# Attention probabilities transposed by VectorE blocks and small transfers instead of TensorE

## The chip, the cores and the metric

The kernel runs on one core of one Trainium2 chip (trn2). The core has five engines with their own instruction streams: TensorE (PE; its weight loads are listed apart as PEld), VectorE (DVE), ScalarE (ACT), GpSimd (POOL) and SyncE (SP), which here only issues transfers. TensorE reads SBUF and writes PSUM. The metric is the device time of one execution in microseconds (us), lower is better; a change counts as faster or slower when it moves that time by over 2%.

## The reference, cut to what matters

There are 64 graphs of 256 nodes with 512 features, all float32, and two layers. Layer 0 is gated attention with 8 heads of 64 channels; layer 1 is a graph attention with one head. The change concerns layer 0.

```python
x:   (64, 256, 512) float32      adj: (64, 256, 256) int32

h = relu(layernorm(x))
q, k, v = (h @ Wq.T), (h @ Wk.T), (h @ Wv.T)          # split into 8 heads of 64
scores = einsum('bqhd,bkhd->bhqk', q, k) / sqrt(64)
scores = where(adj != 0, scores, -inf)
attn = softmax(scores, axis=-1)                       # 256 x 256 per head and graph
c = einsum('bhqk,bkhd->bqhd', attn, v)                # <- needs attn with k on the partitions
gate = sigmoid(concat([c, h]) @ Wg.T + bg)
x = x + gate * h + (1 - gate) * c
# layer 1
h = relu(layernorm(x)); Wh = h @ W
e = leaky_relu(Wh @ a1 + (Wh @ a2).T);  e = where(adj == 0, -1e9, e)
x = x + elu(softmax(e) @ Wh)
```

The softmax runs along a row, so a query lies on a partition and the keys along it. The product with v sums over the keys, so TensorE wants the keys on the partitions: each 256 x 256 matrix of probabilities has to be transposed between the two.

## The kernel before

Projections are done by a seven-product Strassen scheme (products into three PSUM banks `ma`, `mb`, `mc`, added up by VectorE with the help of `u` tiles). The work is pipelined over graphs: round `i` works on the attention of graph `i`, on the projections of graph `p = i+1`, on the gate of graph `q = i-1` and on layer 1 of graphs `q` and `r = i-2`. The order of TensorE and SyncE is the program order; that of the other engines is chosen by a scheduler when the program is built, and is fixed then too. The heads are handled in two halves of four.

```python
sb pools (buffers): ... "e": 4 [128 x 2 x 256], "eT": 4 [128 x 2 x 256], "adj": 1, "h": 1 ...
ps pools (PSUM banks): "ma": 1, "mb": 1, "mc": 1, "w": 5

def to_channels(h, name, pool):                # h of layer 0: VectorE blocks, 16 transfers per graph
    for t in range(NT):
        nc.vector.transpose(h[:, t, :], h[:, t, :])
    ...
    for i in range(0, P, 32):
        for j in range(0, P, 32):
            nc.sync.dma_start(placed[j:j + 32, :, i:i + 32], blocks[i:i + 32, :, j:j + 32])

def a_scores(g, half):                         # 16 TensorE instructions "ps" into 4 banks
    ...
def a_softmax(g, half, jj):                    # two heads; VectorE: scale, mask, row minimum;
    for i in range(2):                         # ScalarE: exp and row sum
        for t in range(NT):
            nc.vector.tensor_tensor_reduce(e[:, t, :], psc[jj, i][:, t, :], mask[:, t, :], ...)
            nc.scalar.activation(e[:, t, :], e[:, t, :], AF.Exp, ...)
    nc.vector.reciprocal(rec, sums)
    for i in range(2):                         # GpSimd: divide by the sum
        for t in range(NT):
            nc.gpsimd.tensor_scalar(es[jj, i][:, t, :], es[jj, i][:, t, :], rec[:, i, t:t + 1], ...)

def transpose_probs(e, pool, name, on_act):    # one head: 4 TensorE transposes, one copy
    pt = ps["w"].tile([P, NT, N], F32, ...)
    for kc in range(NT):
        for t in range(NT):
            nc.tensor.transpose(pt[:, kc, t * P:(t + 1) * P], e[:, t, kc * P:(kc + 1) * P], ident)
    eT = pool.tile([P, NT, N], F32, ...)
    evac(eT, pt, on_act)                       # ScalarE for layer 0

def a_weigh(g, half):                          # "pc": probabilities times v
    for jj in range(2):
        for kc in range(NT):
            for i in range(2):
                nc.tensor.matmul(pc[i * DK:(i + 1) * DK, jj, :], v[...], eT[jj, i][:, kc, :], ...)

def emit_round(i):                             # order of one round, cut
    load_graph(p+1); gate(q) part 0; softmax(i, 0, 1); edges(r); gate(q) part 1; sums(p)
    gate(q) part 2; mix(q); transpose(r); a_transpose(i, 0)
    qk(p) part 0; residual(q); out(r, 0); norm(q); qk(p) part 1
    a_scores(i, 1); softmax(i, 1, 0); out(r, 1); softmax(i, 1, 1); qk(p) part 2
    transpose_h(q); v(p) part 0; a_weigh(i, 0); v(p) part 1; stats(p+1)
    a_transpose(i, 1); v(p) part 2; wh(q) part 0; norm(p+1); p_transpose(p+1)
    a_weigh(i, 1); wh(q) part 1; a_scores(p, 0); softmax(p, 0, 0); wh(q) part 2
```

Tiles and their names in the profile: `ps` scores, `e` probabilities, `ptr` their transposes in PSUM, `eT` the same in SBUF, `pc` the product with v, `hT_l<-h_l` the 16 transfers of `to_channels`, `pma_/pmb_/pmc_` the Strassen banks, `py` and `pt_l` other transposes, `po` the product of layer 1, `S_l`, `S_g`, `S_c` sums of inputs for the Strassen scheme (GpSimd).

Of the kernel before, what the change touches and what calls it, by code (L numbers as in the profile page):

```python
# [8 lines left out]
F32 = mybir.dt.float32  # L9
I32 = mybir.dt.int32  # L10
BF16 = mybir.dt.bfloat16
AF = mybir.ActivationFunctionType
ALU = mybir.AluOpType
# [5 lines left out]
HUGE = 3e38  # L19
# [3 lines left out]
def kernel(  # L23
# [27 lines left out]

    nc = tc.nc
    B, N, H = x.shape
    NH = 8
    DK = H // NH
    P = 128
    HC = H // P
    NT = N // P  # L60
    HH = H // 2
    SCALE = 1.0 / DK ** 0.5
    assert N == 256 and H == 512 and SCALE == 0.125

    def pool(name, bufs, **kw):
        return ctx.enter_context(tc.tile_pool(name=name, bufs=bufs, **kw))
# [1 line left out]
    const = pool("const", 1)  # L68
    st = pool("st", 4)
    sb = {tag: pool(tag, bufs) for tag, bufs in {  # L70
        "x": 5, "adj": 1, "mask": 4, "hT": 3, "S": 3, "qk": 3, "v": 2, "wh": 1, "e": 4, "eT": 4,
        "cT": 1, "z": 1, "h": 1, "tmp": 6, "U": 3,
    }.items()}
    ps = {tag: pool(f"ps_{tag}", bufs, space=bass.MemoryType.PSUM) for tag, bufs in {
        "ma": 1, "mb": 1, "mc": 1, "w": 5,
    }.items()}

    ident = const.tile([P, P], F32, name="ident")
# [21 lines left out]
    def weight_sums(key):  # L100

        w = weight[key]
        t = const.tile([P, 3, 2, w.shape[3]], F32, name=f"w{key}_t")
        b11, b12, b21, b22 = (w[:, r:r + 2, n, :] for r in (0, 2) for n in range(2))
        nc.vector.tensor_tensor(t[:, 1], b22, b12, ALU.subtract)
        nc.vector.tensor_tensor(t[:, 0], t[:, 1], b11, ALU.add)
        nc.vector.tensor_tensor(b12, b12, b11, ALU.subtract)
        nc.vector.tensor_tensor(t[:, 2], b21, t[:, 0], ALU.subtract)
        weight[key] = {1: b11, 2: b21, 3: b22, 4: t[:, 2], 5: b12, 6: t[:, 0], 7: t[:, 1]}
# [21 lines left out]
    def evac(dst, src, on_act):  # L131
        if on_act:
            nc.scalar.copy(dst, src)  # L133
        else:
            nc.vector.tensor_copy(dst, src)  # L135
# [80 lines left out]
    def to_channels(h, name, pool):  # L216


        for t in range(NT):
            nc.vector.transpose(h[:, t, :], h[:, t, :])  # L220
        hT = pool.tile([P, NT, HC, P], F32, tag="t", name=f"hT_{name}")
        blocks = h.rearrange("p t (c q) -> p (t c) q", q=P)
        placed = hT.rearrange("p t c q -> p (t c) q")
# [3 lines that stand above are left out]
        return hT  # L227
# [23 lines left out]

    def p_transpose(g):
        s = graphs[g]
        s["hT"] = to_channels(s.pop("h"), f"l0_{g}", sb["hT"])

    def p_sums(g):
        s = graphs[g]
# [36 lines left out]
    def a_scores(g, half):  # L294
        s = graphs[g]
        qk = s["qk"][half]
        psc = {}
        for jj in range(2):
            for i in range(2):
                psc[jj, i] = ps["w"].tile([P, NT, N], F32, tag="t", name=f"ps_{g}_{half}_{jj}_{i}")  # L300
            for t in range(NT):
                for i in range(2):
                    r = i * DK
                    nc.tensor.matmul(  # L304
                        psc[jj, i][:, t, :], qk[r:r + DK, 0, jj, t * P:(t + 1) * P], qk[r:r + DK, 1, jj, :],
                        start=True, stop=True,
                    )
        s["ps"] = psc

        s["e", half] = {}  # L310

    def a_softmax(g, half, jj):
        s = graphs[g]
        psc, mask, es = s["ps"], s["mask"], s["e", half]
        low, sums, rec = (
            st.tile([P, 2, NT], F32, tag=tag, name=f"{tag}_{g}_{half}_{jj}") for tag in ("low", "sums", "rec")
        )
        for i in range(2):
            e = es[jj, i] = sb["e"].tile([P, NT, N], F32, tag="t", name=f"e_{g}_{half}_{jj}_{i}")
            for t in range(NT):  # L320
                nc.vector.tensor_tensor_reduce(  # L321
                    e[:, t, :], psc[jj, i][:, t, :], mask[:, t, :], -SCALE, HUGE, ALU.add, ALU.min,
                    accum_out=low[:, i, t:t + 1],
                )
                nc.scalar.activation(  # L325
                    e[:, t, :], e[:, t, :], AF.Exp, bias=low[:, i, t:t + 1], scale=-1.0,
                    accum_out=sums[:, i, t:t + 1],
                )
        nc.vector.reciprocal(rec, sums)  # L329
        for i in range(2):  # L330
            for t in range(NT):
                nc.gpsimd.tensor_scalar(  # L332
                    es[jj, i][:, t, :], es[jj, i][:, t, :], rec[:, i, t:t + 1], 1.0, ALU.mult, ALU.mult
                )

    def transpose_probs(e, pool, name, on_act):

        pt = ps["w"].tile([P, NT, N], F32, tag="t", name=f"ptr_{name}")
        for kc in range(NT):
            for t in range(NT):  # L340
                nc.tensor.transpose(pt[:, kc, t * P:(t + 1) * P], e[:, t, kc * P:(kc + 1) * P], ident)  # L341
        eT = pool.tile([P, NT, N], F32, tag="t", name=f"eT_{name}")
        evac(eT, pt, on_act)
        return eT

    def a_transpose(g, half):
        s = graphs[g]
        s["eT", half] = {
            (jj, i): transpose_probs(e, sb["eT"], f"{g}_{half}_{jj}_{i}", 1) for (jj, i), e in s.pop(("e", half)).items()
        }  # L350

    def a_weigh(g, half):
        s = graphs[g]
        eT = s.pop(("eT", half))
        if half == 0:
            s["cT"] = sb["cT"].tile([P, NT, HC, P], F32, tag="t", name=f"cT_{g}")
        pc = ps["w"].tile([P, 2, N], F32, tag="t", name=f"pc_{g}_{half}")
        for jj in range(2):
            for kc in range(NT):
                for i in range(2):  # L360
                    hd = 4 * half + 2 * jj + i
                    nc.tensor.matmul(  # L362
                        pc[i * DK:(i + 1) * DK, jj, :], s["v"][:, kc, hd * DK:(hd + 1) * DK], eT[jj, i][:, kc, :],
                        start=(kc == 0), stop=(kc == NT - 1),
                    )
        evac(
            s["cT"][:, :, 2 * half:2 * half + 2, :].rearrange("p t j q -> p j t q"),
            pc.rearrange("p j (t q) -> p j t q", q=P), 1,
        )
        if half:  # L370
            s["cS"] = token_sums(s["cT"], f"c_{g}")
# [77 lines left out]

    def g_transpose(g):  # L450
        s = graphs[g]
        s["egT"] = transpose_probs(s["eg"], sb["tmp"], f"l1_{g}", 0)

    def g_out(g, t):
        s = graphs[g]
# [17 lines left out]
    def emit_round(i):  # L473


        parts = {}

        def step(fn, g, *args):
            if 0 <= g < B:
                fn(g, *args)  # L480

        def part(fn, g, n):
            if 0 <= g < B:
                if n == 0:
                    parts[fn] = fn(g)
                parts[fn][n]()

        p, q, r = i + 1, i - 1, i - 2
        step(load_graph, p + 1)
        part(g_gate, q, 0)  # L490
        step(a_softmax, i, 0, 1)
        step(g_diff, q)
        step(g_edges, r)
        part(g_gate, q, 1)
        step(p_sums, p)
        part(g_gate, q, 2)
        step(g_mix, q)
        step(g_transpose, r)
        step(a_transpose, i, 0)
        if i == -1:  # L500
            weight_sums("q")
            weight_sums("k")
        part(p_qk, p, 0)
        step(g_residual, q)
        step(g_out, r, 0)
        step(g_norm, q)
        part(p_qk, p, 1)
        step(a_scores, i, 1)
        step(a_softmax, i, 1, 0)
        step(g_out, r, 1)  # L510
        step(a_softmax, i, 1, 1)
        part(p_qk, p, 2)
        step(g_transpose_h, q)
        if i == -1:
            weight_sums("v")
        part(p_v, p, 0)
        step(a_weigh, i, 0)
        if i == 0:
            weight_sums("gh")
            weight_sums("gc")  # L520
            nc.vector.tensor_scalar_mul(hbg, hbg, 0.5)
        part(p_v, p, 1)
        step(p_stats, p + 1)
        step(a_transpose, i, 1)
        part(p_v, p, 2)
        if i == 0:
            edge_columns()
            weight_sums("1")
        part(g_wh, q, 0)
        step(p_norm, p + 1)  # L530
        step(p_transpose, p + 1)
        step(g_sums, i)
        step(a_weigh, i, 1)
        part(g_wh, q, 1)
        step(a_scores, p, 0)
        step(a_softmax, p, 0, 0)
        part(g_wh, q, 2)
# [49 lines left out]
```

## Time and profile before

The time is 3592.71 us, the median of three runs (3591.24 to 3593.61). The profiled execution has a span of 3590.0 us.

| engine | busy, us | share of the span | instructions |
|---|---|---|---|
| PE | 3529.6 | 98% | 25984 |
| PEld | 3072.2 | 86% | 25984 |
| DVE | 1960.6 | 55% | 5673 |
| ACT | 1607.4 | 45% | 4289 |
| POOL | 1626.9 | 45% | 2439 |

The clock granted to TensorE is 0.995 of full speed in the mean, and below nine tenths in the last of 40 slices alone. The 16 DMA engines are busy some 10 to 20% of the time and move 128.74 MB. A page of the profile gives such sums; which engine sets the end is read from the chain of waits, and where the time of one stage goes is read from the timeline of one round. A round is the same sequence 64 times over, with a start and an end in which parts of it are missing.

### The profile page before, as it was taken

The numbers are of one execution on the slowest core, as the hardware profiler recorded it, in microseconds if no ns is written. First come the engines' busy times: TensorE is split into PE (matmuls) and PEld (weight loads), VectorE is DVE, ScalarE is ACT, GpSimd is POOL, SyncE is SP. The second block draws the span as 40 slices with busy tenths as digits, with TensorE's granted clock in tenths as the row PEclk, the third lists the DMA queues.
The fourth block names the chain that finished last, engine by engine and source line by source line (L and its number), as shares of the span: only waits on it lengthen the run. The fifth ranks groups of instructions, "written<-read, shape, count | busy, mean of one in ns | idle before, by whom it ended". The sixth has DMA issues, their size and how long they took to land.

```text
span 3590.0 us, 68740 instructions
## 1 busy us (share of the span) xinstructions
PE 3529.6 (98%) x25984; PEld 3072.2 (86%) x25984; DVE 1960.6 (55%) x5673; ACT 1607.4 (45%) x4289; POOL 1626.9 (45%) x2439
## 2 busy tenths in 40 slices
PE   5999999999999999999999999999999999999997
PEld 5888888888888888888888888888888888888885
DVE  5555555555555555555555555555555555555544
ACT  2444444444444444444444444444444444444443
POOL 3444454354444444543544444445435444444443
PEclk9999999999999999999999999999999999999998
DMA  4111111111110111111111101111111111011100
GB/s 117 28 42 33 31 42 31 33 42 28 36 42 22 42 33 31 42 30 33 42 27 36 42 22 42 33 31 42 31 34 42 28 36 42 22 42 33 31 19 18
DMA packets 338235, 128.74 MB, mean 36 GB/s; under 512 B 282352, under 2 KB 304880, under 8 KB 337904
## 3 DMA queue, kind: packets, MB, share of 16 engines
q1 hardware_dynamic: 336848, 123.29, 13.5%
q8 instruction: 206, 3.38, 0.4%
q14 instruction: 125, 1.02, 0.1%
q10 hardware_dynamic: 1056, 1.05, 0.1%
HBM read 57.15 MB, written 33.55 MB: 25 GB/s over the span
## 4 chain that ended last, share of the span: by engine, by line
PE 97%; DVE 1%; POOL 1%; SPq 1%; DMA 0%; ACT 0%; issue 0%; POOLq 0%; ACTq 0%; DVEq 0%
PE pmb_z L160 10%; PE pmb_qk L160 9%; PE ps L304 7%; PE pc L362 7%; PE po L458 6%; PE pma_z L160 6%; PE pmc_z L160 6%; PE pma_qk L160 6%; PE ptr L341 6%; PE pmc_qk L160 6%; PE pmb_wh L160 5%; PE pmb_v L160 5%; PE pmc_wh L160 3%; PE pma_wh L160 3%; PE pmc_v L160 3%; PE pma_v L160 3%
## 5 line engine op out<-in xcount | busy, mean ns | idle before, releaser
L204 POOL TENSOR_TENSOR rs_l<-ve_l,mhalf 128x2 f32<-128x2 f32 x128 | 90.4, 706 | 1205.1 <-DVE ve_l L202 1205.1
L332 POOL TENSOR_SCALAR e<-e,rec 128x256 f32<-128x256 f32 x1024 | 504.1, 511 | 254.2 <-DVE rec L329 242.3
L325 ACT ACTIVATE e<-e,low 128x256 f32<-128x256 f32 x1024 | 505.6, 495 | 86.4 <-DVE low L321 84.5
L321 DVE CUSTOM_DVE_ANT_0 e<-ps,mask 128x256 f32<-128x256 f32 x1024 | 373.4, 417 | 75.2 <-PE ps L304 73.7
L465 ACT ACTIVATE pos<-po,rec 128x512 f32<-128x512 f32 x128 | 86.6, 677 | 424.0 <-DVE neg L463 424.0
L133 ACT COPY eT<-ptr 128x512 f32<-128x512 f32 x512 | 261.5, 593 | 14.2 <-PE ptr L341 10.1
L341 PE MATMUL ptr<-ident,e 128*128 128x128 f32 x2048 | 248.9, 274 | 10.9 <-POOL e L332 10.5
L304 PE MATMUL ps<-qk 64*128 64x256 f32 x2048 | 255.7, 389 | 0.0
L458 PE MATMUL po<-wh,eT_l 128*128 128x512 f32 x512 | 251.6, 615 | 0.8 <-DVE eT_l L135 0.8
L362 PE MATMUL pc<-eT,v 128*64 128x256 f32 x2048 | 249.3, 385 | 0.0
L341 PEld LDWEIGHTS ptr<-ident,e 128*128 128x128 f32 x2048 | 230.9, 142 | 20.8 <-POOL e L332 14.1
L443 ACT ACTIVATE eg<-eg,nm 128x256 f32<-128x256 f32 x128 | 64.0, 500 | 383.4 <-DVE nm L440 383.4
L213 ACT ACTIVATE h_l<-x,nb_l,rs_l 128x512 f32<-128x512 f32 x256 | 201.8, 813 | 62.3 <-DVE nb_l L210 62.1
L133 ACT COPY cT<-pc 128x512 f32<-128x512 f32 x128 | 74.9, 585 | 345.0 <-PE pc L362 345.0
L304 PEld LDWEIGHTS ps<-qk 64*128 64x128 f32 x2048 | 187.3, 186 | 46.8 <-issue 22.1
L170 DVE TENSOR_TENSOR u_wh<-pmb_wh,u_wh 128x257 f32<-128x257 f32 x128 | 54.6, 427 | 308.7 <-PE pmb_wh L160 308.7
L362 PEld LDWEIGHTS pc<-eT,v 128*64 128x64 f32 x2048 | 135.6, 136 | 97.9 <-issue 42.3
L401 ACT ACTIVATE z<-z,hbg 128x256 f32<-128x256 f32 x256 | 116.3, 501 | 192.3 <-DVE z L170 192.3
L325 ACT ACTIVATION_READ_ACCUMULATOR e<-e,low 128x1 f32 x1024 | 191.5, 187 | 0.0
L468 POOL TENSOR_TENSOR x<-x,pos 128x512 f32<-128x512 f32 x128 | 162.9, 1273 | 61.2 <-DVE nb_l L210 35.7
L170 DVE TENSOR_TENSOR u_qk<-pmb_qk,u_qk 128x512 f32<-128x512 f32 x128 | 88.4, 691 | 166.6 <-PE pmb_qk L160 165.9
L199 DVE BATCH_NORM_STATS2 bs_l<-x 128x6 f32<-128x512 f32 x256 | 166.3, 671 | 17.2 <-DMA x<-in_x_dram 17.2
(144 smaller groups left out, 8494.4 us busy)
## 6 DMA issues: line engine op xcount, KB each, us to landing
x<-in_x_dram SPq DMA_DIRECT2D x64, 512.0 KB, 4.0
hT_l<-h_l SPq DMA_DIRECT2D x1024, 32.0 KB, 2.0
out_dram<-x SPq DMA_DIRECT2D x64, 512.0 KB, 2.8
adj<-in_adj_dram SPq DMA_DIRECT2D x64, 256.0 KB, 4.0
wk_sb<-in_L_gnn_Wk_dram ACTq DMA_DIRECT2D x2, 512.0 KB, 6.8
wq_sb<-in_L_gnn_Wq_dram SPq DMA_DIRECT2D x2, 512.0 KB, 8.7
wv_sb<-in_L_gnn_Wv_dram SPq DMA_DIRECT2D x2, 512.0 KB, 10.3
wgh_sb<-in_L_gnn_Wg_dram SPq DMA_DIRECT2D x2, 512.0 KB, 5.2
```

Of the source, the lines that this page charges most:

```text
L133: nc.scalar.copy(dst, src)
L160: nc.tensor.matmul(bank[key][(slice(None), *cols)], lhsT, rhs, start=first and i == 0, stop=last and i == len(todo) - 1, skip_group_check= ...
L199: nc.vector.bn_stats(bs, xt[:, t, :])
L213: nc.scalar.activation(h[:, t, :], xt[:, t, :], AF.Relu, bias=nb[:, t:t + 1], scale=rs[:, t:t + 1])
L304: nc.tensor.matmul(psc[jj, i][:, t, :], qk[r:r + DK, 0, jj, t * P:(t + 1) * P], qk[r:r + DK, 1, jj, :], start=True, stop=True,)
L321: nc.vector.tensor_tensor_reduce(e[:, t, :], psc[jj, i][:, t, :], mask[:, t, :], -SCALE, HUGE, ALU.add, ALU.min, accum_out=low[:, i, t:t + 1],
L325: nc.scalar.activation(e[:, t, :], e[:, t, :], AF.Exp, bias=low[:, i, t:t + 1], scale=-1.0, accum_out=sums[:, i, t:t + 1],)
L332: nc.gpsimd.tensor_scalar(es[jj, i][:, t, :], es[jj, i][:, t, :], rec[:, i, t:t + 1], 1.0, ALU.mult, ALU.mult)
L341: nc.tensor.transpose(pt[:, kc, t * P:(t + 1) * P], e[:, t, kc * P:(kc + 1) * P], ident)
L362: nc.tensor.matmul(pc[i * DK:(i + 1) * DK, jj, :], s["v"][:, kc, hd * DK:(hd + 1) * DK], eT[jj, i][:, kc, :], start=(kc == 0), stop=(kc == ...
L458: nc.tensor.matmul(pm, s["egT"][:, kc, t * P:(t + 1) * P], s["wh"][:, kc, :, :HH], start=(kc == 0), stop=(kc == NT - 1))
L468: nc.gpsimd.tensor_tensor(s["x"][:, t, :], s["x"][:, t, :], pos, ALU.add)
```

## The change

The change takes the transposes of the layer 0 probabilities away from TensorE. VectorE transposes all 32 x 32 blocks of a half (four heads), and writes them grouped by the block row they belong to after the transposition, so that what has to move from one group of 32 partitions to another lies in one run of 2 KB per partition. Then 16 transfers on the SyncE queue put the groups in place, each 32 partitions by 2 KB (64 KB). The copies from PSUM by ScalarE go away with the transposes. The product with v reads its operand through an access pattern of three dimensions (runs of 32 floats), as the blocks of a row now lie 2 KB apart.

The probabilities of a half, their blocks and the placed blocks are tiles of 8 KB per partition, and all three come from one pool of two buffers (before: four of 2 KB and four of 2 KB, the same total). The order of the round is rewritten, so that the transposed probabilities are asked for later after their scores than before. For the first graph alone, `h` is transposed by TensorE and not by VectorE and transfers. The transposes in layer 1 stay on TensorE.

```diff
-        "x": 5, ... "wh": 1, "e": 4, "eT": 4,
+        "x": 5, ... "wh": 1, "e": 2,
@@ p_transpose
-        s["hT"] = to_channels(s.pop("h"), f"l0_{g}", sb["hT"])
+        s["hT"] = (to_channels if g else to_channels_pe)(s.pop("h"), f"l0_{g}", sb["hT"])
@@ a_scores
-        s["e", half] = {}
+        s["e", half] = sb["e"].tile([P, 2, 2, NT, N], F32, tag="t", name=f"e_{g}_{half}")
@@ a_transpose
-        s["eT", half] = {
-            (jj, i): transpose_probs(e, sb["eT"], f"{g}_{half}_{jj}_{i}", 1) for (jj, i), e in ...
-        }
+        e = s.pop(("e", half)).rearrange("p j i t (k b c) -> p (j i) (t k) b c", k=NT, c=32)
+        blocks, eT = (sb["e"].tile([P, 4, 8 * NT, 32], F32, tag="t", ...) for n in ("eb", "eT"))
+        for h in range(4):
+            nc.vector.transpose(
+                blocks[:, :, 4 * h:4 * h + 4, :].rearrange("p b n c -> p n b c"), e[:, h]
+            )
+        for i in range(4):
+            for j in range(4):
+                nc.sync.dma_start(eT[32 * j:32 * j + 32, i], blocks[32 * i:32 * i + 32, j])
+        s["eT", half] = eT.rearrange("p a (h t k) c -> p h k t a c", h=4, t=NT)
@@ a_weigh
-                        pc[i * DK:(i + 1) * DK, jj, :], v[...], eT[jj, i][:, kc, :],
+                        pc[i * DK:(i + 1) * DK, jj, :].rearrange("p (t a c) -> p t a c", t=NT, c=32),
+                        v[...], eT[:, 2 * jj + i, kc],
@@ emit_round
         part(g_gate, q, 1)
         step(p_sums, p)
+        step(a_transpose, i, 0)
         part(g_gate, q, 2)
         step(g_mix, q)
         step(g_transpose, r)
-        step(a_transpose, i, 0)
         part(p_qk, p, 0)
         step(g_residual, q)
         step(g_out, r, 0)
+        step(a_scores, i, 1)
         step(g_norm, q)
+        step(a_softmax, i, 1, 0)
         part(p_qk, p, 1)
-        step(a_scores, i, 1)
-        step(a_softmax, i, 1, 0)
-        step(g_out, r, 1)
+        step(a_weigh, i, 0)
         step(a_softmax, i, 1, 1)
         part(p_qk, p, 2)
         step(g_transpose_h, q)
+        step(a_transpose, i, 1)
         part(p_v, p, 0)
-        step(a_weigh, i, 0)
+        step(g_out, r, 1)
         part(p_v, p, 1)
         step(p_stats, p + 1)
-        step(a_transpose, i, 1)
         part(p_v, p, 2)
         part(g_wh, q, 0)
         ...                                     # norm(p+1), p_transpose(p+1), a_weigh(i, 1), ...
```

More of the change, by code (lines that the diff above doesn't have):

```diff
@@ L70 @@
     sb = {tag: pool(tag, bufs) for tag, bufs in {
-        "x": 5, "adj": 1, "mask": 4, "hT": 3, "S": 3, "qk": 3, "v": 2, "wh": 1, "e": 4, "eT": 4,
+        "x": 5, "adj": 1, "mask": 4, "hT": 3, "S": 3, "qk": 3, "v": 2, "wh": 1, "e": 2,
         "cT": 1, "z": 1, "h": 1, "tmp": 6, "U": 3,
@@ L308, in a_scores @@
         s["ps"] = psc
-        s["e", half] = {}
+        s["e", half] = sb["e"].tile([P, 2, 2, NT, N], F32, tag="t", name=f"e_{g}_{half}")
     def a_softmax(g, half, jj):
         s = graphs[g]
-        psc, mask, es = s["ps"], s["mask"], s["e", half]
+        psc, mask, es = s["ps"], s["mask"], s["e", half][:, jj]
         low, sums, rec = (
@@ L318, in a_softmax @@
         for i in range(2):
-            e = es[jj, i] = sb["e"].tile([P, NT, N], F32, tag="t", name=f"e_{g}_{half}_{jj}_{i}")
             for t in range(NT):
                 nc.vector.tensor_tensor_reduce(
-                    e[:, t, :], psc[jj, i][:, t, :], mask[:, t, :], -SCALE, HUGE, ALU.add, ALU.min,
+                    es[:, i, t, :], psc[jj, i][:, t, :], mask[:, t, :], -SCALE, HUGE, ALU.add, ALU.min,
                     accum_out=low[:, i, t:t + 1],
@@ L325, in a_softmax @@
                 nc.scalar.activation(
-                    e[:, t, :], e[:, t, :], AF.Exp, bias=low[:, i, t:t + 1], scale=-1.0,
+                    es[:, i, t, :], es[:, i, t, :], AF.Exp, bias=low[:, i, t:t + 1], scale=-1.0,
                     accum_out=sums[:, i, t:t + 1],
@@ L332, in a_softmax @@
                 nc.gpsimd.tensor_scalar(
-                    es[jj, i][:, t, :], es[jj, i][:, t, :], rec[:, i, t:t + 1], 1.0, ALU.mult, ALU.mult
+                    es[:, i, t, :], es[:, i, t, :], rec[:, i, t:t + 1], 1.0, ALU.mult, ALU.mult
                 )
[L336 to L344, printed above, removed]
     def a_transpose(g, half):
         s = graphs[g]
-        s["eT", half] = {
-            (jj, i): transpose_probs(e, sb["eT"], f"{g}_{half}_{jj}_{i}", 1) for (jj, i), e in s.pop(("e", half)).items()
-        }
+        e = s.pop(("e", half)).rearrange("p j i t (k b c) -> p (j i) (t k) b c", k=NT, c=32)
+        blocks, eT = (sb["e"].tile([P, 4, 8 * NT, 32], F32, tag="t", name=f"{n}_{g}_{half}") for n in ("eb", "eT"))
+        for h in range(4):
[6 more added lines that the diff above has]
+        s["eT", half] = eT.rearrange("p a (h t k) c -> p h k t a c", h=4, t=NT)
     def a_weigh(g, half):
@@ L362, in a_weigh @@
                     nc.tensor.matmul(
-                        pc[i * DK:(i + 1) * DK, jj, :], s["v"][:, kc, hd * DK:(hd + 1) * DK], eT[jj, i][:, kc, :],
+                        pc[i * DK:(i + 1) * DK, jj, :].rearrange("p (t a c) -> p t a c", t=NT, c=32),
+                        s["v"][:, kc, hd * DK:(hd + 1) * DK], eT[:, 2 * jj + i, kc],
                         start=(kc == 0), stop=(kc == NT - 1),
@@ L451, in g_transpose @@
         s = graphs[g]
-        s["egT"] = transpose_probs(s["eg"], sb["tmp"], f"l1_{g}", 0)
+        e = s["eg"]
+        pt = ps["w"].tile([P, NT, N], F32, tag="t", name=f"ptr_{g}")
+        for kc in range(NT):
+            for t in range(NT):
+                nc.tensor.transpose(pt[:, kc, t * P:(t + 1) * P], e[:, t, kc * P:(kc + 1) * P], ident)
+        s["egT"] = sb["tmp"].tile([P, NT, N], F32, tag="t", name=f"egT_{g}")
+        evac(s["egT"], pt, 0)
     def g_out(g, t):
```

## The prediction

> **What bounds the kernel now.** I read the page's busy shares first, then the chain that ended last, then the costliest groups.
>
> ```profile
> PE 3529.6 (98%) x25984; PEld 3072.2 (86%) x25984; DVE 1960.6 (55%) x5673; ACT 1607.4 (45%) x4289; POOL 1626.9 (45%) x2439
> ...
> PE 97%; DVE 1%; POOL 1%; SPq 1%; DMA 0%; ACT 0%; issue 0%; POOLq 0%; ACTq 0%; DVEq 0%
> ...
> L332 POOL TENSOR_SCALAR e<-e,rec 128x256 f32<-128x256 f32 x1024 | 504.1, 511 | 254.2 <-DVE rec L329 242.3
> ...
> L133 ACT COPY eT<-ptr 128x512 f32<-128x512 f32 x512 | 261.5, 593 | 14.2 <-PE ptr L341 10.1
> L341 PE MATMUL ptr<-ident,e 128*128 128x128 f32 x2048 | 248.9, 274 | 10.9 <-POOL e L332 10.5
> ```
>
> A busy share alone would not do, but the chain is 97% TensorE too: it almost never waits, and the time is the sum of what it is given. So anything taken from TensorE's stream shortens the kernel, until something makes it wait. The last row is what the change takes away: 2048 transposes (64 graphs x 8 heads x 4). Their 274 ns overlap, so their worth is read from the pace, in TensorE's timeline of one round:
>
> ```profile
> 1803.25 0.60 PE L341 MATMUL ptr_l<-ident,eg 128*128 128x128 f32 x4
> 1803.68 1.91 PE L341 MATMUL ptr<-ident,e 128*128 128x128 f32 x16
> 1805.43 1.06 PE L160 MATMUL pma_qk<-hT_l,wq_sb 128*128 128x128 f32 x8
> ```
>
> The columns are start, duration, instruction. From 1803.68 to the next block's start is 1.75 us for 16 transposes (one half of a graph). A round (from the gate's first product at 1790.53 to the next at 1845.39) is 54.86 us without a listed wait, and 64 of them are 3511 of the 3590 us.
>
> **What the Trainium skill says.** "VectorE: DVE Perf Modes", section "The three transpose paths": VectorE transposes 32 x 32 blocks only, so the rest is left to placing; the layer 0 `h` is done so in this trace, at 710 ns for 128 x 512. "DMA: Bandwidth & Descriptors", section "Anatomy of one DMA": a transfer has about 2 us of fixed cost, mostly until its landing is confirmed; the trace agrees, 2.0 us for the 16 small `hT_l` transfers. "SBUF — State Buffer", section "Who interferes with whom": a VectorE instruction with one SBUF input does not contend with GpSimd, so the new transposes should not slow the division on GpSimd; no run so far shows it. "TensorE: Matmul & The Clock Gate", section "Why this matters for your kernels": idle gaps above some 3 us cost TensorE its clock. Here even less did, near the end:
>
> ```profile
> 3521.24 2.26 PE L341 MATMUL ptr<-ident,e 128*128 128x128 f32 x8 [1.82 <-POOL e L332]
> ```
>
> Eight transposes took 2.26 us after 1.82 us of waiting, against 1.06 us in the steady stretch. A long wait in every round would thus cost more than itself.
>
> **The change part by part.**
>
> 1. Removed from TensorE: two blocks of 1.75 us per round, 3.49 us x 64 = 223 us, all on the path. The round becomes 51.37 us of TensorE work.
>
> 2. Removed from ScalarE: 512 copies, 261.5 us, beside other work. Worth nothing by itself.
>
> 3. Added to VectorE: 4 transposes of 128 x 512 per half, 512 in all. By the row of the transposes already there
>
> ```profile
> L220 DVE STREAM_TRANSPOSE h_l<-h_l 128x512 f32<-128x512 f32 x128 | 90.8, 710 | 57.0 <-ACT h_l L213 57.0
> ```
>
> that is 512 x 710 ns = 364 us, VectorE at about 2320 us of some 3400 (68%). Not the bound as a sum, but its order is fixed, and a transpose that waits for GpSimd holds up what stands behind it.
>
> 4. Added to SyncE: 2048 issues. What one costs decides the case. The present 16 take
>
> ```profile
> 1828.58 11.34 SPq L226 DMA_DIRECT2D hT_l<-h_l  x16
> 1839.97 0.60 SPq L88 DMA_DIRECT2D x<-in_x_dram  x1
> 1840.61 0.47 SPq L89 DMA_DIRECT2D adj<-in_adj_dram  x1
> ```
>
> or 0.71 us each, each cut into 256 runs of 128 bytes. Simpler ones alone took 0.38 (the store of `out`, in the same round), 0.44 to 0.47 (`x` at the start, `adj`). The new ones are 32 runs of 2 KB with plain rows on both sides, so I choose 0.48 us, and call anything from 0.40 to 0.71 possible. The bytes are not the limit: `x`, 512 KB, lands in 4.0 us, so with 2 us fixed 64 KB is 0.25 us. SyncE would be busy 2 x 7.7 + 11.3 + 1.5 = 28 us of a round.
>
> 5. The first graph's `h` goes through TensorE. Its first product waits now until 27.93 us for the small transfers; `h` is ready at 13.8 us, 8 transposes and two copies later is about 16.5, but the sums for the second product (4 x 0.72 us on GpSimd) bring it to about 20. I count 9 us saved. At the other end, the last round with attention has little TensorE work between scores and product (7 us after the `ps` block), and the new path is over 20 us long: 10 to 13 us lost where some 3 are lost now. I take the two as cancelling.
>
> **Do the transposed halves arrive in time?** I laid the new order on the measured paces; t = 0 is the start of the gate. TensorE: gate and `pe` 12.7, `ptr` of layer 1 0.43, six `qk` blocks 5.36, `py` 0.87, `po` 1.73; so the second half's scores start at 21.1. Then scores 2.0, four `qk` blocks 3.6: the first half's product `pc` is due at 26.8, the second's at 43.7.
>
> First half: its scores start at -3.9. The last row sums came 5.8 us after the scores' start in the old timeline, the GpSimd divisions end about 8.5 us after it, so VectorE has its blocks ready near 5.3. SyncE may still be at the `hT` transfers and loads until 6. 16 x 0.48 + 2.0 gives 15.7, at worst (0.71) 19.4. Due at 26.8: hidden by 7 us or more. The same transfers must also have read their blocks before the second half's softmax writes that buffer (two buffers for `e`, blocks and `eT`), from 23 on: met.
>
> Second half, in the order that the built program has on each engine: VectorE is held by the residual and statistics until 23.1; one instruction waits for GpSimd's power (0.7 us), another there until about 30.7 because the power stands behind four divisions; the last reciprocal is at 30.8; four divisions (0.47 us each) end at 32.9, the fourth transpose at 33.7. Landing: 33.7 + 15 x pitch + 2.0, which is 42.9 at 0.48, 44.7 at 0.60, 46.3 at 0.71. Due at 43.7. Besides, VectorE frees the `pmb` bank only after those transposes, at 34.4, where TensorE wants it at 34.0: 0.4 us lost anyway. So I get **a wait of 0.4 us per round at 0.48, 1.0 at 0.60, 2.6 and a lower clock at 0.71**. I add 0.2 us for the first half's transposes, which stand in front of a gate addition that TensorE needs at 5.6.
>
> Sum: 3592.7 - 223 + 64 x 0.6 = 3408, rounded up to 3412 for the wider spread upward.
>
> **The rivals.** (a) *Issue time takes the place of the transposes.* At the pitch of the existing transfers the wait eats 2.6 of the 3.49 us, and with slower matmuls after it 3 or more: 3550 to 3600. For it: the same queue and loop; against: eight times fewer runs per transfer, and `x` with 256 runs took only 0.44. (b) *VectorE's fixed order becomes the bound*: transposes waiting for GpSimd hold back the freeing of banks, TensorE waits at several places for 0.3 to 1 us. 68% busy speaks against a full stop, the order for some of it: 3440 to 3500. (c) *The operand in runs of 32 floats slows the product.* It takes 249 us now; 10% would be 25 us. Nothing in this trace shows such an operand. (d) *All hidden*, also the small waits: 3592.7 - 223 = 3370.
>
> **Range and chances.** The low end is (d), 3372. The high end allows a pitch near 0.66 us or (b) with some of (c): 3530. Faster by over 2% means below 3521; I give 0.78, as it takes a wait below about 2.4 us per round. Within 2%: 0.15, rival (a). Slower by over 2%, above 3665, needs a wait of over 4.6 us: 0.07, for what I do not see, as a queue that backs up.
>
> **What would show it.** The `ptr` group gone except for layer 1's, and a round of 51.4 us plus waits. The SyncE timeline: 16 transfers in 7 to 8 us (step 4), in 11 if rival (a) is right. Waits of TensorE for the `eT` transfers: none at the first half's product, few tenths at the second's (step on arrival). VectorE's new transposes at 710 ns (step 3). The pace of `pc`, 1.88 us per block, unchanged (rival c). Waits of TensorE for VectorE at `pmb` below 0.5 us (rival b). First product near 16 to 17 us (step 5). I would be wrong if the transfers take over 0.6 us each, or if small lags of VectorE, GpSimd and ScalarE add up from round to round, as each half's chain begins only when TensorE has made its scores.

## The result and the profile after

The changed kernel takes 3486.02 us, the median of four runs (3484.76 to 3486.95), against 3592.32 before: a ratio of 0.9704, with a 95% interval of 0.9687 to 0.9721. It is faster by 3.0%, 106 us, where 180 us were predicted.

The page of the changed kernel, from the busy shares, the chain that ended last and the groups (there: busy, mean ns of one, then idle time of the engine before them and its releaser):

```profile
PE 3324.3 (95%) x23944; PEld 2865.9 (82%) x23944; DVE 2294.7 (66%) x6184; ACT 1338.4 (38%) x3778; POOL 1637.9 (47%) x2439
...
PE 59%; SPq 16%; DVE 12%; POOL 4%; DMA 4%; issue 3%; ACT 1%; DVEq 0%; POOLq 0%; ACTq 0%
SPq L349 16%; PE pmb_z L162 10%; PE pma_z L162 6%; PE pmc_z L162 6%; PE pmb_qk L162 6%; PE pc L362 5%; PE ps L306 5%; PE pma_qk L162 5%; PE pmc_qk L162 4%; PE pmb_wh L162 4%; DMA eT<-eb 4%; DVE e L322 2%; POOL e L333 2%; DVE bs_l L201 2%; PE pma_wh L162 2%
...
L344 DVE STREAM_TRANSPOSE eb<-e 128x512 f32<-128x512 f32 x512 | 345.6, 694 | 88.4 <-POOL e L333 88.3
L362 PE MATMUL pc<-eT,v 128*64 128x256 f32 x2048 | 259.0, 396 | 111.7 <-DMA eT<-eb 103.0
```

TensorE's busy share alone, 95%, would still name it as the bound. The chain says otherwise: it is TensorE for only 59%, and for 16% it is SyncE's queue at line 349, the issue of the new transfers. The last row names the place: TensorE idles in front of `pc` until `eT` has landed. It happens in every round, as TensorE's timeline of one shows (start, duration, in brackets the idle time before and its releaser):

```profile
1825.12 1.03 PE L162 MATMUL pmc_wh<-w_sb,S_l 128*128 128x257 f32 x4
1827.46 1.95 PE L362 MATMUL pc<-eT,v 128*64 128x256 f32 x16 [1.32 <-DMA eT<-eb]
```

and what SyncE and VectorE did before it, from the timelines of both in that round:

```profile
1812.69 0.16 DVE L212 SCALAR_TENSOR_TENSOR nb_l<-mv_l,rs_l 128x2 f32<-128x2 f32 x1 [0.98 <-POOL rs_l L206]
...
1814.92 0.71 DVE L344 STREAM_TRANSPOSE eb<-e 128x512 f32<-128x512 f32 x1 [0.20 <-POOL e L333]
```
```profile
1815.70 10.01 SPq L349 DMA_DIRECT2D eT<-eb  x16
1825.95 0.39 SPq L477 DMA_DIRECT2D out_dram<-x  x1
```

The fourth transpose ends at 1815.63, SyncE starts 70 ns later and needs 10.01 us for 16 issues, 0.63 us each. The last is issued near 1825.1; with 2.0 us to landing that is 1827.1, and the product starts at 1827.46. It was due at 1826.09 (`pmc_wh` takes 0.87 us to its successor, and a change of tile shape 0.1).

Where the 105.4 us between the two profiled spans (3590.0 and 3484.6) come from, cut at the starts of the gates of single graphs:

| stretch | before, us | after, us | difference |
|---|---|---|---|
| to the first graph's gate | 93.7 | 90.7 | -3.0 |
| 61 rounds | 3342.7 (54.80 each) | 3232.8 (53.00 each) | -109.9 |
| the two rounds after | 96.3 | 105.9 | +9.6 |
| the rest | 57.2 | 55.1 | -2.1 |

### The profile page after: what moved, and what is told of

Read it like the earlier page. It is cut to its first block, busy times and chain, and to the rows that moved or that the text cites. A ratio compares the mean times of both kernels' runs of the same rounds, so it can differ in the third digit from the quotient of the medians.

```text
span 3484.6 us, 68023 instructions
## 1 busy us (share of the span) xinstructions
PE 3324.3 (95%) x23944; PEld 2865.9 (82%) x23944; DVE 2294.7 (66%) x6184; ACT 1338.4 (38%) x3778; POOL 1637.9 (47%) x2439
## 4 chain that ended last, share of the span: by engine, by line
PE 59%; SPq 16%; DVE 12%; POOL 4%; DMA 4%; issue 3%; ACT 1%; DVEq 0%; POOLq 0%; ACTq 0%
SPq L349 16%; PE pmb_z L162 10%; PE pma_z L162 6%; PE pmc_z L162 6%; PE pmb_qk L162 6%; PE pc L362 5%; PE ps L306 5%; PE pma_qk L162 5%; PE pmc_qk L162 4%; PE pmb_wh L162 4%; DMA eT<-eb 4%; DVE e L322 2%; POOL e L333 2%; DVE bs_l L201 2%; PE pma_wh L162 2%
## 5 line engine op out<-in xcount | busy, mean ns | idle before, releaser
L333 POOL TENSOR_SCALAR e<-e,rec 128x256 f32<-128x256 f32 x1024 | 473.7, 482 | 256.0 <-DVE rec L330 133.5
L344 DVE STREAM_TRANSPOSE eb<-e 128x512 f32<-128x512 f32 x512 | 345.6, 694 | 88.4 <-POOL e L333 88.3
L362 PE MATMUL pc<-eT,v 128*64 128x256 f32 x2048 | 259.0, 396 | 111.7 <-DMA eT<-eb 103.0
L362 PEld LDWEIGHTS pc<-eT,v 128*64 128x64 f32 x2048 | 150.9, 140 | 193.4 <-issue 115.2
L465 PE MATMUL po<-wh,egT 128*128 128x512 f32 x512 | 245.8, 603 | 0.8 <-DVE egT L137 0.8
L148 POOL TENSOR_TENSOR S_l<-hT_l 128x256 f32<-128x256 f32 x128 | 93.7, 732 | 166.5 <-DVE hT_l L137 166.5
L146 POOL TENSOR_TENSOR S_c<-cT 128x256 f32<-128x256 f32 x64 | 46.4, 725 | 255.2 <-ACT cT L135 255.2
L393 POOL TENSOR_TENSOR d<-hT_l,cT 128x512 f32<-128x512 f32 x128 | 162.5, 1270 | 0.0
```

The lines of the kernel that those rows point to most:

```text
L333: nc.gpsimd.tensor_scalar(es[:, i, t, :], es[:, i, t, :], rec[:, i, t:t + 1], 1.0, ALU.mult, ALU.mult)
L344: nc.vector.transpose(blocks[:, :, 4 * h:4 * h + 4, :].rearrange("p b n c -> p n b c"), e[:, h])
L362: nc.tensor.matmul(pc[i * DK:(i + 1) * DK, jj, :].rearrange("p (t a c) -> p t a c", t=NT, c=32), s["v"][:, kc, hd * DK:(hd + 1) * DK], eT[ ...
L465: nc.tensor.matmul(pm, s["egT"][:, kc, t * P:(t + 1) * P], s["wh"][:, kc, :, :HH], start=(kc == 0), stop=(kc == NT - 1))
```

## The experiments

Theory A: the number of issues on SyncE's queue decides when the second half arrives. Rivals: B, the bytes decide it; C, VectorE's fixed order decides it.

**Half the issues, the same bytes** (left out: the placing that completes the transpose; the blocks go to other places):

```diff
-        for i in range(4):
+        for i in range(2):
             for j in range(4):
-                nc.sync.dma_start(eT[32 * j:32 * j + 32, i], blocks[32 * i:32 * i + 32, j])
+                nc.sync.dma_start(eT[64 * i:64 * i + 64, j], blocks[64 - 64 * i:128 - 64 * i, j])
```

> Leaves out the right placing: the same bytes per half, but as 8 transfers of 64 partitions by 2 KB instead of 16 of 32 partitions, to places that are not those of the transpose. Theory A (the number of issues on the SyncE queue, 0.63 us each, sets when the second half arrives): 8 issues take about 5 us instead of 10, the wait of 1.35 us per round at the second product goes, the round is 51.4 us, the time about 3390 us (3375 to 3410). Theory B (the bytes, or the landing of so many of them, set it): the 16 destinations still get the same bytes, so the wait stays and the time is 3486 us within 10. Theory C (VectorE's order is what comes last): unchanged too.

Measured: 3527.52 us, slower than the changed kernel (ratio to before 0.982, 0.9805 to 0.9835), so all three theories missed the time. SyncE's timeline, however, has what A says, 8 issues of 128 KB in 4.96 us, 0.62 each:

```profile
1792.71 4.96 SPq L349 DMA_DIRECT2D eT<-eb  x8
```

The wait before `pc` is left at the two ends only (9.0 us in all). In its place the list of waits (in total, times, longest) has

```profile
DVE mask L247 <- DMA adj<-in_adj_dram: 130.6, 60, 5.1
...
PE pmb_z L162 <- DVE u_z L172: 114.1, 60, 4.5
```

VectorE waits for the adjacency of the next graph, and TensorE 1.9 us per round for an addition that stands behind it on VectorE. Two things did this. The adjacency is loaded behind the store of `out`, the 16 transfers of `h` and `x`, and the store starts when the residual of layer 1 is done (SyncE waits 368 us for it in all), not when SyncE is free. And in this program the scheduler had put the mask two places earlier, ahead of that addition; in the changed kernel it stands behind it.

**Half the bytes, the same issues** (the product reads two heads twice, so half of the attention is left out):

```diff
-                nc.sync.dma_start(eT[32 * j:32 * j + 32, i], blocks[32 * i:32 * i + 32, j])
+                nc.sync.dma_start(eT[32 * j:32 * j + 32, i, :4 * NT], blocks[32 * i:32 * i + 32, j, :4 * NT])
-                        ... eT[:, 2 * jj + i, kc],
+                        ... eT[:, i, kc],
```

> Leaves out half of the data: 16 transfers per half as in the changed kernel, but 1 KB per partition instead of 2, and the product reads the first two heads twice. Theory A (number of issues): 0.63 us each as before, wait of 1.35 us unchanged, the time 3486 us within 10. Theory B (bytes): half of the bytes, the last lands earlier, the wait shrinks by a microsecond or more per round, about 3400 to 3420 us.

Measured: 3488.32 us (0.9718, 0.9702 to 0.9734), the time of the changed kernel. A round is 53.06 us, against 53.00: the way to the second product is 0.12 us shorter in the mean, and the mask, two places earlier in this program too, costs 0.25 us at the gate. The issues of 32 KB take as long as those of 64, by SyncE's timeline and the list of waits of this run:

```profile
1816.65 10.02 SPq L349 DMA_DIRECT2D eT<-eb  x16
```
```profile
PE pc L362 <- DMA eT<-eb: 99.8, 62, 7.8
```

That rules B out: 32, 64 and 128 KB cost 0.63, 0.63 and 0.62 us in a row. The bytes count only at the end of the row: from issue to landing the three take 1.8, 2.0 and 2.8 us in the median.

**Four of the 16 issued by ScalarE:**

```diff
+                eng = nc.scalar if i == 3 else nc.sync
-                nc.sync.dma_start(...)
+                eng.dma_start(...)
```

> The same transfers, but the four whose source is the last group of 32 partitions are issued by ScalarE, the other twelve by SyncE. Theory A: SyncE is done 4 x 0.63 = 2.5 us earlier, more than the wait of 1.35 us; round 51.4 to 51.7 us, time 3390 to 3415 us, unless ScalarE, which has to wait in its fixed order for VectorE's blocks, holds up its own copies (then 3420 to 3470). Theory B or C (bytes, a limit shared by all queues, or VectorE's order): 3486 us or more.

Measured: 3526.66 us (0.9825, 0.981 to 0.984). By the time alone this would speak for B or C, but it has the picture of the first experiment: the wait at `pc` only at the ends, the mask waiting 111.9 us for the adjacency and TensorE 97.8 us for the addition behind it.

**The new transposes in the old order of the round:**

> VectorE's transposes and the 16 transfers as changed, but the order of the round as it was before the change. Less TensorE work lies between the second half's scores (t = 24.7) and its product (t = 43.6), and VectorE's second transposes stand behind an addition that needs a product at 38.3. By theory A they end near 39.5, the last lands near 51.6: a wait of 8 us per round, and a lower clock after it; round 59 to 61 us, time 3850 to 4000 us. If the transposes themselves were the whole gain and the order only a detail, it would be near 3486 us.

Measured: 4049.34 us, 12.8% slower than before (1.1277, 1.126 to 1.1293), somewhat above the range given. One round of TensorE's timeline:

```profile
1818.55 3.68 PE L362 MATMUL pc<-eT,v 128*64 128x256 f32 x16 [8.42 <-DMA eT<-eb]
1822.16 1.51 PE L162 MATMUL pmb_wh<-w_t,S_l 128*128 128x257 f32 x4
```

The wait is the 8 us worked out beforehand. It costs more than itself: after it the product takes 3.68 us instead of 1.95, and the next block 1.51 instead of 1.14; the granted clock is 0.931 in the mean of the run. The reordering is not a detail but what makes this way of transposing pay.

**The adjacency loaded early, alone:**

```diff
+        step(load_adj, p + 2)              # ahead of the 16 transfers of h
         step(p_transpose, p + 1)           # load_graph at the start of the round loads x only
```

> The changed kernel with one thing moved: the adjacency of the graph after next is loaded ahead of the 16 small transfers of h, not behind them and behind x, so some 12 us earlier. The changed kernel itself doesn't wait for it, so by theory A (number of issues of the second half) the wait of 1.35 us per round stays and the time is 3486 us within 12. If the late adjacency were what costs the changed kernel its gain, it would fall to about 3400.

Measured: 3507.11 us (0.977, 0.9755 to 0.9784), 21 us more than the changed kernel, not the same as expected. The wait at `pc` stays (107.4 us, 103 in the changed kernel). The mask is two places earlier here too, so the addition `u_z`, which frees a bank for TensorE, comes later:

```profile
1801.60 0.95 DVE L252 TENSOR_SCALAR mask<-adj 128x512 bf16<-128x512 int32 x1
1802.46 0.67 DVE L446 TENSOR_REDUCE nm<-eg 128x2 f32<-128x512 f32 x1
1803.06 0.41 DVE L177 TENSOR_TENSOR u_z<-pmb_z,u_z 128x256 f32<-128x256 f32 x1
```
```profile
1802.41 1.06 PE L167 MATMUL pma_z<-cT,wgc_sb 128*128 128x128 f32 x8
1803.52 1.16 PE L167 MATMUL pmb_z<-hT_l,wgh_t 128*128 128x128 f32 x8
1804.52 1.06 PE L167 MATMUL pmb_z<-cT,wgc_t 128*128 128x128 f32 x8
```

From start to start these two gate products take 1.11 and 1.00 us; in the changed kernel they take 0.89 and 0.90. That is 0.32 us per round, some 20 us in the 61 rounds (53.33 us each, against 53.00) and so nearly all of the 21. The list of waits has only 6.1 us of it. That the adjacency is not what holds the changed kernel back is plain.

**Half the issues, and the adjacency early** (the placing left out again):

> Leaves out the right placing: 8 transfers of 64 partitions per half, as in e1_wide, with the adjacency loaded early. In e1_wide the wait for the second half was gone and another had come: VectorE stood at the mask until the adjacency landed, and TensorE waited 1.9 us per round for an addition behind it. Theory A: with both out of the way a round is 51.4 us, the time about 3395 us (3380 to 3415). If issues were not the cause and e1_wide only moved a fixed loss about, it would stay above 3470.

Measured: 3393.63 us (0.945, 0.9436 to 0.9464), as A said. 61 rounds take 51.68 us each, against 53.00 in the changed kernel and 51.37 of TensorE work. The run that it has to be compared with is the one just before, which differs in the issues alone and takes 53.33 us per round: VectorE, ScalarE and GpSimd have the same order in both, and the fourth transpose of the second half ends 33.80 us into the round in both (means of 57 rounds), but the last transfer lands at 40.7 instead of 45.5. This settles it, and C falls too. What is left over the 51.37 us is the late addition at the gate, 0.3 us per round as before.

**Four by ScalarE, and the adjacency early** (nothing is left out):

> The same transfers, four of the 16 of each half issued by ScalarE, and the adjacency loaded early. Theory A: round 51.4 to 51.7 us, time 3395 to 3415 us. Rival: ScalarE's issues (0.6 us each, and a wait for VectorE's blocks in its fixed order) hold up its own copies, 3420 to 3470.

Measured: 3423.84 us (0.9535, 0.9519 to 0.9551), 1.8% less than the changed kernel, and in the rival's range. A round is 52.13 us. The wait at `pc` is left at the ends only (14.1 us in all), here with the transpose complete. SyncE's and ScalarE's timelines show both rows of issues side by side:

```profile
1786.20 8.00 SPq L355 DMA_DIRECT2D eT<-eb  x12
```
```profile
1786.17 1.80 ACTq L355 DMA_DIRECT2D eT<-eb  x3
1788.07 0.58 ACT L140 COPY hT_l<-pt_l 128x512 f32<-128x512 f32 x1 [5.39 <-DVE hT_l L142]
1788.08 0.54 ACTq L355 DMA_DIRECT2D eT<-eb  x1
1788.66 0.37 ACT L181 COPY u_v<-pma_v 128x256 f32<-128x256 f32 x1
```

Twelve take 8.00 us and four 2.45 at the same time, so the pace belongs to each queue and is not shared. Of the 0.76 us over 51.37, 0.43 are the late addition at the gate. The other 0.34 are the rival's mechanism: ScalarE's copy `u_v` stands behind the issues and comes 1.8 us later in the round than in the run above, VectorE's addition waits for it and what follows on VectorE comes late, so TensorE gets a bank late at the products for v:

```profile
1789.07 0.42 DVE L177 TENSOR_TENSOR u_v<-pmb_v,u_v 128x256 f32<-128x256 f32 x1 [1.16 <-ACT u_v L181]
```

**The four groups that stay in their partitions copied by ScalarE:**

```diff
+                if i == j:
+                    nc.scalar.copy(eT[32 * j:32 * j + 32, i], blocks[32 * i:32 * i + 32, j])
+                else:
                     nc.sync.dma_start(...)
```

> The four block groups that stay in their own 32 partitions are copied by ScalarE (32 partitions by 512), the other twelve are transferred as before, adjacency early. Theory A: SyncE issues 12 instead of 16 per half, 2.5 us less, more than the 1.35 us wait; round 51.4 to 51.7 us, time 3395 to 3415 us. Rival: eight copies per round, 0.5 to 0.6 us each, hold up ScalarE's other copies: 3420 to 3470.

Measured: 3464.46 us (0.9649, 0.9634 to 0.9663), the rival rather than the hope. ScalarE's timeline has the copies in one block ahead of its work for the next products, and the list of waits where it is paid:

```profile
1809.47 2.50 ACT L355 COPY eT<-eb 32x512 f32<-32x512 f32 x4 [3.49 <-DVE eb L349]
...
1813.32 0.35 ACT L181 COPY u_v<-pma_v 128x256 f32<-128x256 f32 x1
```
```profile
PE pmb_v L167 <- DVE u_v L177: 47.9, 62, 2.5
```

**The first graph's `h` by small transfers, as before the change:**

```diff
-        s["hT"] = (to_channels if g else to_channels_pe)(s.pop("h"), f"l0_{g}", sb["hT"])
+        s["hT"] = to_channels(s.pop("h"), f"l0_{g}", sb["hT"])
```

> The changed kernel with one part undone: the first graph's h goes through VectorE blocks and 16 small transfers like all others. The first gate product started 3.0 us earlier in the changed kernel than before the change, where 9 us were predicted for the start. If the transposes by TensorE are what gained at the start, undoing them costs 9 to 12 us (the small transfers need 11 us): 3495 to 3500 us. If the gain of the first product is lost again in the first round's wait for the transposed probabilities (8.3 us there), it costs 0 to 4 us: 3486 to 3490.

Measured: 3505.83 us (0.9766, 0.975 to 0.9782), 20 us more than the changed kernel and outside both ranges. The first product comes at 28.0 us instead of 16.8, and the first gate at 104.6 instead of 90.7, so this part is worth 13.9 us at the start. The other 6 us lie in the 61 rounds (53.10 us each, 53.00). The order of the engines in them is the same, but the wait at `pc` is a little longer and the granted clock falls after it in six rounds instead of four; why is not shown.

**ScalarE in the second half alone:**

> Adjacency early, and four of the 16 transfers issued by ScalarE in the second half alone; the first half has time to spare and stays on SyncE with all 16. By theory A the wait for the second half stays away, and ScalarE no longer stands still at the gate, where it waited 213 us in f2_act4_adj: round 51.4 to 51.8 us, time 3400 to 3418 us. Rival: the first half's later end (2.5 us) makes the second half's softmax wait for its buffer, 3420 or more.

Measured: 3423.69 us (0.9534, 0.952 to 0.9549), the same as with both halves; the round stays at 52.14 us. The time is in the rival's range, but TensorE's round shows the same two delays as before (0.43 and 0.32 us), so the first half's end is not the reason; the four issues in the second half, which both programs have, remain. The reading behind the expectation was wrong. The wait of 213 us lies at `eg`, the exponential of layer 1's edges, not at the gate, and the lists of the two runs show that only its name changed, not its sum (first two lines: issues in both halves; last line: in one):

```profile
ACT eg L450 <- DVE nm L447: 214.8, 33, 7.1
ACT eg L450 <- DMA eT<-eb: 212.8, 31, 7.1
```
```profile
ACT eg L450 <- DVE nm L447: 428.9, 64, 7.1
```

**The same, with two halves at the ends transposed by TensorE:**

```diff
+        if (g, half) in ((0, 0), (B - 1, 1)):
+            ...                            # 16 TensorE transposes, copies by ScalarE and VectorE
```

> As g1_act_half, and two halves are transposed by TensorE as before the change: the first half of the first graph and the second half of the last, where TensorE has little else to do and waited 8.2 and 6.0 us for the transfers in f2_act4_adj. 32 transposes cost 3.5 us and replace these waits and the low clock after them: 6 to 12 us less than g1_act_half, so 3390 to 3410 us.

Measured: 3416.26 us (0.9515, 0.9501 to 0.953), 7 us less, and the fastest version that leaves nothing out: 4.9% faster than before, and some 2% less than the changed kernel, at the edge of what counts as faster. Most of the gain lies in the two rounds at the end (94.0 us instead of 101.5). The first gate comes only 1.2 us earlier, as the transposes there wait for GpSimd's division instead (6.4 us). Its chain is TensorE's again:

```profile
PE 91%; DVE 6%; POOL 1%; issue 1%; ACT 1%; SPq 0%; DMA 0%; ACTq 0%; POOLq 0%; DVEq 0%
```

## Why the prediction was right, and where it was off

**Direction and mechanism: right.** The `ptr` transposes were worth what they took, and what the change gives back is a wait at the second half's product, where the prediction looked for it. The replay of a round held closely (t = 0 at 1782.29): scores at 21.2 (21.1 said), first product at 26.9 (26.8) without a wait in the steady rounds, fourth transpose at 33.3 (33.7), second product due at 43.8 (43.7).

**Step 4, the issue: the term that was mis-sized.** 0.48 us per issue was chosen, from transfers issued alone; in a row they take 0.63, as half and double sizes show. The prediction's own sum, 33.3 + 15 x 0.63 + 2.0 = 44.8, gives a wait of 1.0 us. The remaining 0.4 us of the measured 1.4 are 0.07 us before the first issue and 0.34 us between the last landing and the product, which the sum leaves out. The reason given for 0.48, fewer and longer runs, does not hold: the 256 runs of 128 bytes take 0.71 us, the 32 of 2 KB 0.63. The 2.0 us to the landing held, though the section named for them describes transfers issued by GpSimd, and these are issued by SyncE. By the prediction's own sign, over 0.6 us each, this step was wrong; that the time still falls where it was expected is owed to a range wide enough for 0.66.

**The 0.6 us per round: none of it came.** At 0.48 the sum had no wait for the transfers at all (42.9 against 43.7). Its 0.6 us were 0.4 for the `pmb` bank, freed late, and 0.2 for a gate addition behind the first half's transposes. VectorE's and TensorE's timelines show both additions done in time, the first at 1787.61 for a bank wanted at 1787.86, the second at 1816.21 for one wanted at 1816.48:

```profile
1787.22 0.39 DVE L172 TENSOR_TENSOR u_z<-pmb_z,u_z 128x256 f32<-128x256 f32 x1
...
1815.56 0.65 DVE L172 TENSOR_TENSOR qk<-pmb_qk,u_qk 128x512 f32<-128x512 f32 x1
```
```profile
1787.86 1.06 PE L162 MATMUL pmb_z<-S_g,wgh_t 128*128 128x128 f32 x8
...
1816.48 1.03 PE L162 MATMUL pmb_v<-wv_t,S_l 128*128 128x256 f32 x4
```

So two losses that did not come stood in for part of one that did, which is luck.

**The sum.** A round was to be 51.97 us and is 53.00: 1.03 us over 61 rounds is 63 us of the 74 us by which the prediction was low. Nearly all of the 1.63 us over 51.37 lie at the second product. From the start of `pmc_wh` to that of `pc` TensorE takes 2.48 us in the mean of the 61 rounds, against 0.96 in the run with half the issues and the adjacency early. The other 0.1 us are the product and the block after it, which were slow in the four rounds with the longest waits.

**Step 5, the ends: a wrong size on one side.** The TensorE transposes of the first graph are worth 13.9 us, not 9. But the waits of 8.3 and 5.0 us for the first graph's two halves, and a slow product after each (3.68 and 3.55 us), take most back, and 3.0 us are left at the first gate; the prediction had no term for them. The loss at the end, 9.6 us, was foreseen as 7 to 10. The two do not quite cancel: with the last stretch of the table (2.1 us gained) 4.5 us of loss are left.

**Steps 1 to 3: right.** VectorE is at 2295 us (2320 said), and a transpose takes 694 ns on average (710). GpSimd's division takes 482 ns in the mean, 511 before, so no slowing by the new transposes shows. That ScalarE's saving is worth nothing was not tested; before the change TensorE waited 4.9 us in all for ScalarE.

**The rivals.** (a) came true in part: the pitch is much nearer to that of the small transfers than to the one chosen. (b) was small in the changed kernel, but it is what held the experiments back as soon as the transfers came in time. (c) is ruled out by the timeline: a block of `pc` still takes 1.88 us to its successor (1809.19 to 1811.07), with its operand in runs of 32 floats. A low clock after a wait, expected for long ones, did not follow the usual 1.4 us here. It did follow 8 us, and 2.1 to 2.6 us in four of the 61 rounds, as in this one, where the granted clock was 0.50 from 3099.3 to 3102.5:

```profile
3098.96 3.53 PE L362 MATMUL pc<-eT,v 128*64 128x256 f32 x16 [2.53 <-DMA eT<-eb]
```

The prediction's own example, 2.26 us for eight transposes after 1.82 us, is partly misread: the clock was still 1.00 for the first 1.3 us of them and 0.50 only from 3522.6 to 3525.9, and the 1.06 us that it was compared with are those of eight products, not of transposes.

## What to carry to other kernels

When work moves from a full engine to many small transfers, count the issues before the bytes: here a row of transfers of 32 to 128 KB cost its number times the issue time of its queue, measured in a row and not alone. Then lay the new chain, from producer through issues to landing, against the work that stands between in the order of the bound engine; the reordering that makes room for it can be worth more than the transposes themselves. And after one wait is taken away, look for the next at once: here a late load, and a scheduler that had put its reader two places earlier, hid the whole gain of the right remedy. So compare an experiment with the run that has the same order on every engine.

## What the runs showed of the hardware that was not expected

- Issues on SyncE in a row took 0.62 to 0.63 us each whether they moved 32, 64 or 128 KB; the same queue issued a 512 KB store alone in 0.39 us. Four on ScalarE's queue took 2.45 us while SyncE issued its own twelve.
- ScalarE's copy of 32 partitions by 512 took 617 ns, as long as one of 128 partitions by 512 (577 to 593 ns). The former read SBUF and the latter PSUM, so the number of partitions is not the only difference.
- VectorE's block transposes with a result scattered in runs of 32 floats at 2 KB steps were no slower (694 ns) than those in place (710 ns).
